# Two projections of a graph attention layer: both made with features on the partitions, values turned back through DRAM

## The chip, the cores and the metric

The kernel runs on one core of one Trainium2 chip. The metric is the device time of one execution in microseconds (us), taken as the median of several runs. A hardware profile of one execution lists the work of each engine: TensorE (PE, with its weight loads as PEld), VectorE (DVE), ScalarE (ACT), GpSimd (POOL) and SyncE (SP), which only issues transfers here.

## The reference, cut to what matters

x is 3327 x 512, adj a 0/1 matrix of 3327 x 3327, W_stack two matrices of 512 x 1024.

```
def gat_layer(x, W, adj):
    Wh, Ws = split(x @ W, 2, axis=-1)        # W = [Wa | Wb]: Wh = x Wa, Ws = x Wb
    a = softmax(Wh @ Ws.T, axis=-1) * adj
    return leaky_relu(a @ Wh + x, 0.01)
y = gat_layer(gat_layer(x, W_stack[0], adj), W_stack[1], adj)
x = layernorm(x + y)
xw = (x > 0) @ sign(weight).T                # then support = adj
x = layernorm(x + relu(adj @ xw))
```

Wh serves twice: as the queries of the scores (Wh Ws^T) and as the values (a Wh). The scores can also be written x (Wa Wb^T) x^T, and the kernel before does so: M = Wa Wb^T is made once for a layer, x itself is the keys, and M applied to x is the queries.

## The kernel before, in words

**Tiles.** The 3327 rows are 26 tiles of 128, taken as 13 pairs (`q`) and as 7 chunks (`c`) of four tiles; the last chunk has two. The 512 features are four groups of 128. Everything in the attention layers is fp32, and one fp32 matmul is two records in the profile. Products of 2x2 blocks are made by the seven-product scheme of Strassen: `seven` (L169) gives seven closures of one chain, each with a product into one of three PSUM banks (X, Y, Z), copies by ScalarE and three additions by VectorE. It needs sums of blocks of both factors: `left_sums` (L204) and `right_sums` (L211), four additions each, S1 to S4 and T1 to T4.

**project (L320)**, for each layer, in three kinds of work per chunk:
- values, Wh with rows on the partitions: x^T is the stationary operand and Wa moves (L408). The result stays in SBUF as `wh[q]`; its sums (`ws_d`) are stored to DRAM by POOL.
- keys: blocks of x^T and their sums (`key_sums`, L236), stored to DRAM as `xs_d` by POOL.
- queries, with features on the partitions: M times x^T (L464); for the half chunk at the end directly, without the scheme (L442). Stored as `gs_d`.

M is made by `product_m` (L304): 16 matmuls of 128x512. It needs Wa and Wb with features of the other side on the partitions. In layer 0 TensorE transposes them at the start of project (`transpose_w`, L257); for layer 1 `load_w_laid` and `turn_w` (VectorE, L283) do it at the end of attention 0.

x of later chunks comes by `load_laid` (L129: four DMAs of 64 KB a tile) and is turned to x^T by VectorE (`turn_x`, L231). The first chunk of layer 0 is transposed by TensorE (L348).

**Order.** A helper `weave` merges lists of closures, each spread evenly. Tiles named `slot` come from one ring of 33 buffers (tag `s`). SP's queue carries all loads in program order, POOL's queue the stores. PSUM has 8 banks: `ch` 3, `acc` 4, `tr` 1.

**attention (L556)** takes 169 steps (g, q) per layer. Scores run 30 steps ahead (`LOOK`), so the last 17 steps have no scores: only the values' products (L822, 7 matmuls a step), with VectorE's shift, running sum and mask (L741, L752, L757) and POOL's sums (L795 to L798). The dictionary `early` places other work by step; toward the end of attention 0 it places the loads and the turning of layer 1's W, M of layer 1 (in the last 14 steps), and the turning of the first chunk of layer 1's x. In steps before 0 the scores' look-ahead runs alone. After layer 1 come the last aggregation and the final normalization.

Of the kernel before, what the change touches and what calls it, by code (L numbers as in the profile page):

```python
# [19 lines left out]
P = 128  # L20
CT = 4
# [9 lines left out]
def kernel(  # L31
# [71 lines left out]
    ba_d = tc.dram_tile([NT, P, D], BF16, name="ba_d")  # L103
    xw_d = tc.dram_tile([NT, P, D], F16, name="xw_d")
# [60 lines left out]

    S1, S2, A11, A12, A21, A22, S3, S4 = range(8)
    B11, B21, B22, T4, T1, T2, T3 = range(7)

    def seven(lane, name, multiply, c11, c12, c21, c22):  # L169
# [5 lines left out]
        def product(i, b, start):  # L175
            if start:
                bank[b] = pool.tile([P, HW], F32, tag=tag, name=f"p{b}_{name}")
            multiply(i, bank[b], start)

        def copied(i, b):  # L180
            if not held:
                two = slot([P, 2, HW], F32, f"h0_{name}"), slot([P, 2, HW], F32, f"h1_{name}")
                held.update(zip(("p1", "p5", "u2", "u3"), (t[:, e] for t in two for e in (0, 1))))
            nc.scalar.copy(held[i], bank[b])
# [19 lines left out]
    def left_sums(a11, a12, a21, a22, s1, s2, s3, s4, eng=nc.vector, between=lambda: None):  # L204
        eng.tensor_tensor(s1, a21, a22, ALU.add)
        eng.tensor_tensor(s2, s1, a11, ALU.subtract)
        between()
        eng.tensor_tensor(s3, a11, a21, ALU.subtract)
        eng.tensor_tensor(s4, a12, s2, ALU.subtract)

    def right_sums(b11, b12, b21, b22, t1, t2, t3, t4):  # L211
        nc.vector.tensor_tensor(t1, b12, b11, ALU.subtract)
        nc.vector.tensor_tensor(t2, b22, t1, ALU.subtract)
        nc.vector.tensor_tensor(t3, b22, b12, ALU.subtract)
        nc.vector.tensor_tensor(t4, b21, t2, ALU.subtract)
# [10 lines left out]
    ch_lane, acc_lane, tr_lane = (ps_ch, "ch"), (ps_acc, "acc"), (ps_tr, "tr")  # L226
    w_rows, w_laid, wT, m_of, wsum_of, x_first, keys_first = ({} for _ in range(7))
# [8 lines left out]
    def key_sums(l, q, a, xT, between=lambda: None):  # L236

        j1, j2 = ts(2 * a, P), ts(2 * a + 1, P)
        s12 = slot([P, 2, 2, P], F32, f"s12_{l}_{q}")
        s34 = slot([P, 2, 2, P], F32, f"s34_{l}_{q}")  # L240
        of = {
            A11: xT[:, 0:2, j1], A12: xT[:, 2:4, j1], A21: xT[:, 0:2, j2],
            A22: xT[:, 2:4, j2], S1: s12[:, 0], S2: s12[:, 1], S3: s34[:, 0],
            S4: s34[:, 1], "s12": s12, "s34": s34,
        }
        left_sums(
            *(of[i] for i in (A11, A12, A21, A22, S1, S2, S3, S4)), between=between
        )
        return of

    def load_w(l, h):

        for k in range(KD):
# [3 lines left out]
    def transpose_w(l, h, k, lane):  # L257
        pool, tag = lane
        pt = pool.tile([P, D], F32, tag=tag, name=f"pwT_{l}_{h}_{k}")
        for d in range(KD):  # L260
            nc.tensor.transpose(pt[:, ts(d, P)], w_rows[l, h, d][:, ts(k, P)], ident)
        wT[l, h, k] = slot([P, D], F32, f"wTs_{l}_{h}_{k}")
        nc.scalar.copy(wT[l, h, k], pt)

    def load_w_laid(l, h, t):

        wt = w_laid[l, h, t] = slot([P, KD, P], F32, f"wl{h}_{l}_{t}")
        for a in range(P // B):
            nc.sync.dma_start(
                out=wt[ts(a, B)],  # L270
                in_=w_stack[l, ts(t, P), h * D + a * P : h * D + (a + 1) * P].rearrange(
                    "(v r) f -> v r f", r=KD
                ),
            )

    def turn_w(l, h, t):

        if t == 0:
            for k in range(KD):
                wT[l, h, k] = slot([P, D], F32, f"wTs_{l}_{h}_{k}")  # L280
        wt = w_laid.pop((l, h, t))
        for k in range(KD):
            nc.vector.transpose(  # L283
                wT[l, h, k].rearrange("p (r c) -> p r c", c=P)[:, :, ts(t, B)],
                wt[:, :, ts(k, B)],
            )

    def sums_w(l):


        wsum_of[l] = ops.tile([P, 4, 2, HD], F32, tag="gs", name=f"wsum_{l}")

        def part(k, half):
            lo, hi = w_rows[l, 0, k], w_rows[l, 0, 2 + k]
            b11, b12, b21, b22 = lo[:, :HD], lo[:, HD:], hi[:, :HD], hi[:, HD:]
            t1, t2, t3, t4 = (wsum_of[l][:, i, k] for i in range(4))
            for to, x1, x2 in ((t1, b12, b11), (t2, b22, t1)) if half == 0 else (
                (t3, b22, b12), (t4, b21, t2)
            ):
                nc.vector.tensor_tensor(to, x1, x2, ALU.subtract)  # L300

        return [lambda k=k, half=half: part(k, half) for half in range(2) for k in range(2)]

    def product_m(l, lane):  # L304

        pm = {}

        def one(d, k):
            if k == 0:
# [5 lines left out]
            if k == KD - 1:  # L315
                copy_out(d, m_of[l][d // 2][:, d % 2], pm[d])
# [1089 lines left out]
```

## Time and profile before

| | |
|---|---|
| median of three runs | 2601.63 us (2599.69 to 2602.28) |
| the profiled execution | 2600.38 us |
| span of the profile | 2598.5 us |
| granted TensorE clock | 0.999 |
| TensorE busy | 2569.2 us, 99% |
| weight loads busy | 2232.3 us, 86% |
| VectorE busy | 2102.4 us, 81% |
| POOL busy | 1102.9 us, 42% |
| ScalarE busy | 789.1 us, 30% |
| DMA | 642.56 MB, mean 247 GB/s |

How to read the lines that follow. A row of the groups has the line of the kernel, the engine, the operation, output and inputs with shapes, the count, then the busy time, the mean duration of one in ns, and the idle time ahead of it with what ended it. A row of the waits has the engine and instruction that waited, what for, and the time in total, how often, and the longest. A row of the timeline has start and duration of a run of equal instructions. A row of the windows has start and end, length, busy time (and count) of PE, PEld, DVE, ACT and POOL, the granted clock as a share, the DMA's busy share, and GB/s. A row of the DMA issues ends with the KB of one and the median us from issue to landing. Layer 0's value products run from 7.6 us of the span to about 185, layer 1's end at about 1392.

### The profile page before, as it was taken

To read this page: it belongs to the slowest core of one execution; us is meant where nothing else is said; L and a number is where in the kernel's file an instruction comes from. 1 tells how busy PE (TensorE), PEld (TensorE's weight loads), DVE (VectorE), ACT (ScalarE), POOL (GpSimd) and SP (SyncE) were. 2 spreads that over 40 slices of the span, in tenths; PEclk is the share of its full clock that TensorE was granted. 3 is DMA by queue.
4 is the path that set the end of the run, shared out by engine and by line. 5 is a ranking of instruction groups with operands and counts; after the bars stand their busy time and mean duration, and the time that the engine had idled before them with its cause. 6 is when DMAs were issued, how large, how long until landed. Compare 5 with 4: busy or idle time off the path is not lost. (4 is left out here: it accounts for less than half of the span.)

```text
span 2598.5 us, 40105 instructions
## 1 busy us (share of the span) xinstructions
PE 2569.2 (99%) x12423; PEld 2232.3 (86%) x12448; DVE 2102.4 (81%) x4442; ACT 789.1 (30%) x1956; POOL 1102.9 (42%) x2048
## 2 busy tenths in 40 slices
PE   9999999999999999999999999999999999999998
PEld 7888888888888888887888888888888888888787
DVE  6756889889898888768875878888888888877976
ACT  3323333333333333221333333333333333222143
POOL 3640344444444444546652144444444444455611
PEclk9999999999999999999999999999999999999999
DMA  6857777877777777787866877777777777778775
GB/s 216 295 193 231 246 247 232 268 235 259 251 240 251 239 247 235 233 259 250 307 235 208 249 239 259 251 258 244 266 258 258 247 256 251 243 261 277 264 247 186
DMA packets 329992, 642.56 MB, mean 247 GB/s; under 512 B 48921, under 2 KB 189555, under 8 KB 329516
## 3 DMA queue, kind: packets, MB, share of 16 engines
q1 hardware_dynamic: 293020, 530.82, 63.1%
q0 software_dynamic: 36752, 109.10, 11.2%
q8 instruction: 102, 1.67, 0.3%
q14 instruction: 118, 0.97, 0.1%
HBM read 530.22 MB, written 109.55 MB: 246 GB/s over the span
## 5 line engine op out<-in xcount | busy, mean ns | idle before, releaser
L588 PE MATMUL pZ<-gs,xs 128*128 128x256 f32 x2496 | 636.1, 379 | 1.3 <-ACT u L605 0.7
L588 PEld LDWEIGHTS pZ<-gs,xs 128*128 128x128 f32 x2496 | 473.6, 190 | 67.5 <-ACT u L605 1.1
L795 POOL TENSOR_TENSOR as<-s 128x128 f32<-128x128 f32 x338 | 161.8, 479 | 846.3 <-DVE s L757 669.4
L822 PE MATMUL acc<-ws,s 128*128 128x256 f32 x1352 | 402.1, 379 | 0.0
L822 PE MATMUL acc<-wh,s 128*128 128x256 f32 x1352 | 355.9, 379 | 0.7 <-DVE s L757 0.4
L822 PE MATMUL acc<-ws,as 128*128 128x256 f32 x1352 | 347.9, 380 | 4.8 <-POOL as L797 4.7
L588 PE MATMUL pY<-gs,xs 128*128 128x256 f32 x1248 | 320.4, 379 | 0.0
L747 ACT ACTIVATE s<-s 128x512 f32<-128x512 f32 x338 | 213.4, 631 | 282.9 <-DVE s L741 281.6
L822 PEld LDWEIGHTS acc<-ws,as 128*128 128x128 f32 x1352 | 256.1, 190 | 46.1 <-POOL as L797 8.9
L822 PEld LDWEIGHTS acc<-wh,s 128*128 128x128 f32 x1352 | 256.5, 190 | 36.9 <-DVE s L757 2.2
L822 PEld LDWEIGHTS acc<-ws,s 128*128 128x128 f32 x1352 | 256.0, 190 | 34.5
L588 PEld LDWEIGHTS pY<-gs,xs 128*128 128x128 f32 x1248 | 236.9, 190 | 32.6 <-ACT p L605 0.3
L658 DVE TENSOR_TENSOR top<-top,s 128x512 f32<-128x512 f32 x286 | 198.9, 710 | 80.9 <-ACT s L645 51.7
L741 DVE TENSOR_TENSOR s<-s,off 128x512 f32<-128x512 f32 x338 | 248.1, 734 | 0.5
L757 DVE TENSOR_TENSOR s<-s,adj 128x512 f32<-128x512 f32 x338 | 238.8, 706 | 8.4 <-DMA adj<-in_adjT_dram 0.5
L752 DVE TENSOR_TENSOR total<-total,s 128x512 f32<-128x512 f32 x312 | 230.3, 738 | 0.0
L605 ACT COPY u<-pZ 128x256 f32<-128x256 f32 x312 | 115.9, 371 | 357.2 <-PE pZ L588 356.6
L797 POOL TENSOR_TENSOR as<-s 128x128 f32<-128x128 f32 x338 | 200.6, 594 | 26.5
L822 PE MATMUL acc<-wh,as 128*128 128x256 f32 x676 | 201.2, 379 | 0.0
L796 POOL TENSOR_TENSOR s<-s 128x128 f32<-128x128 f32 x338 | 187.0, 553 | 27.3
L798 POOL TENSOR_TENSOR as<-s,as 128x128 f32<-128x128 f32 x338 | 178.2, 527 | 26.5
L630 DVE TENSOR_TENSOR s<-p,u 128x256 f32<-128x256 f32 x156 | 66.1, 424 | 143.9 <-ACT u L605 143.3
(224 smaller groups left out, 3866.8 us busy)
## 6 DMA issues: line engine op xcount, KB each, us to landing
ws<-ws_d SPq DMA_DIRECT2D x338, 512.0 KB, 3.7
xs<-xs_d SPq DMA_DIRECT2D x182, 512.0 KB, 6.0
adj<-in_adjT_dram SPq DMA_DIRECT2D x315, 256.0 KB, 4.3
xs<-xs_d SPq DMA_DIRECT2D x156, 384.0 KB, 6.5
gs_d<-gsp POOLq DMA_DIRECT2D x88, 256.0 KB, 3.1
gs<-gs_d SPq DMA_DIRECT2D x74, 256.0 KB, 5.2
adj_d<-ab POOLq DMA_DIRECT2D x169, 112.0 KB, 4.1
ahl<-adj_d SPq DMA_DIRECT2D x78, 224.0 KB, 4.6
```

Of the source, the lines that this page charges most:

```text
L588: nc.tensor.matmul(ch[bank], xs[c, q, a][:, k], gs[c][:, b, k], start=(start and k == 0), stop=(k == 1), skip_group_check=True,)
L605: nc.scalar.copy(ch[name], ch[bank])
L658: nc.vector.tensor_tensor(top[i], top[i], t, ALU.max)
L741: nc.vector.tensor_tensor(s, s, off[g].to_broadcast([P, 2, HW]), ALU.subtract)
L747: nc.scalar.activation(sc[g, q], sc[g, q], AF.Exp)
L752: nc.vector.tensor_tensor(total[g], total[g], sc[g, q], ALU.add)
L757: nc.vector.tensor_tensor(s, s, adj[g, q], ALU.mult)
L795: nc.gpsimd.tensor_tensor(s3, a11, a21, ALU.subtract)
L796: nc.gpsimd.tensor_tensor(a21, a21, a22, ALU.add)
L797: nc.gpsimd.tensor_tensor(s2, a21, a11, ALU.subtract)
L798: nc.gpsimd.tensor_tensor(s4, a12, s2, ALU.subtract)
L822: nc.tensor.matmul(acc[g][i // 2][:, i % 2], a[i], b[i], start=(q == 0 and i % 2 == 0), stop=(q == NQ - 1), skip_group_check=True,)
```

## The change

M is no longer made. Both halves of x W are made with features on the partitions: W's blocks are the stationary operand and x^T moves (`products`, called for `wsT`, the keys, and then for `whT`, the queries). Each call is two chains of seven products, 28 matmuls, over all columns of a chunk; in the last chunk the four blocks are 128 columns wide instead of 256 (`width`). ScalarE puts W's columns into the order that the blocks need (`part_w`), VectorE makes W's sums. Keys are blocks of Ws^T with their sums, queries Wh^T with theirs.

The values are the same numbers as the queries, but needed with rows on the partitions. `turn_rows` turns each tile by two VectorE transposes of 128x256 into a buffer `wr` (three copies), from which four DMAs on SP store it to a new DRAM tensor `wh_d`. Later three DMAs on SP load it into `wh[q]` (`load_values`), and VectorE makes its sums: for the first six pairs within project (at chunks 2 to 4), for the other seven in attention's steps −29 to −3. At the start of layer 0 the loads of x and W alternate. For layer 1, Wb is loaded, ordered and summed in the last steps of attention 0; the work with M, and the turning of W, leave those steps.

`left_sums` and `right_sums` now return lists of closures. The diff, cut to its core (of removed functions only the first lines and those that are named here; the rest of project's old loop is left out):

```diff
+    wh_d = [tc.dram_tile([NT, P, D], F32, name=f"wh_d{l}") for l in range(L)]
...
-    def transpose_w(l, h, k, lane):
...
-            nc.tensor.transpose(pt[:, ts(d, P)], w_rows[l, h, d][:, ts(k, P)], ident)
-        wT[l, h, k] = slot([P, D], F32, f"wTs_{l}_{h}_{k}")
-        nc.scalar.copy(wT[l, h, k], pt)
...
-    def load_w_laid(l, h, t):
...
-    def turn_w(l, h, t):
...
-    def product_m(l, lane):
...
-            nc.tensor.matmul(
-                pm[d], wT[l, 0, k][:, ts(d, P)], wT[l, 1, k], start=(k == 0), stop=(k == KD - 1)
-            )
...
+    def part_w(l, h, k, to):
+        nc.scalar.copy(
+            to.rearrange("p (e c) -> p e c", c=P),
+            w_rows.pop((l, h, k)).rearrange("p (c e) -> p e c", e=KD),
+        )
+    def left(lo, hi, sums):
+        of = {A11: lo[:, :, :HD], A12: hi[:, :, :HD], A21: lo[:, :, HD:], A22: hi[:, :, HD:]}
+        of.update({i: sums[:, e] for e, i in enumerate((S1, S2, S3, S4))})
+        return of
+    def left_w(of):
+        return left_sums(*(of[i] for i in (A11, A12, A21, A22, S1, S2, S3, S4)))
+    def width(c):
+        return HW if len(halves_of(c)) == 2 else P
+    def right_x(c, xT, t):
+        w = width(c)
+        lo, hi = xT[:, 0:2], xT[:, 2:4]
+        of = {B11: lo[:, :, :w], B21: hi[:, :, :w], B22: hi[:, :, w : 2 * w]}
+        of.update({i: e[:, :, :w] for i, e in zip((T1, T2, T3, T4), t)})
+        return of, right_sums(
+            of[B11], lo[:, :, w : 2 * w], *(of[i] for i in (B21, B22, T1, T2, T3, T4))
+        )
+    def load_values(l, q, b12):
+        nc.sync.dma_start(out=wh[q][:, 0], in_=wh_d[l][2 * q][:, :HD])
+        nc.sync.dma_start(
+            out=wh[q][:, 1:3], in_=wh_d[l][2 * q + 1].rearrange("p (a n) -> p a n", a=2)
+        )
+        nc.sync.dma_start(out=b12, in_=wh_d[l][2 * q][:, HD:])
...
+        def sums_x(c):
+            if c < 2 or c == NC - 1:
+                t = [slot([P, 2, HW], F32, f"xt_{l}_{c}_{i}") for i in range(4)]
+            else:
+                if "one" not in spare:
+                    spare["one"] = ops.tile([P, 2, HW], F32, tag="xs1", name=f"xt_{l}")
+                units = [spare_of[l][:, 2 * i : 2 * i + 2] for i in range(7)] + [spare["one"]]
+                t = units[:4] if c % 2 == 0 else units[4:]
+            of_x[c], do = right_x(c, xTs[c], t)
+            return do
+        spare = {}
+        wa = pre.tile([P, KD, D], F32, tag="wa", bufs=1, name=f"wa_{l}")
+        m = pre.tile([P, KD, D], F32, tag="m", bufs=1, name=f"wb_{l}")
+        asum = pre.tile([P, 4, 2, HD], F32, tag="msum", bufs=1, name=f"wasum_{l}")
...
+            load_x(0, (0, 1))
+            load_w(l, 1, (0, 1))
+            load_x(0, (2, 3))
+            load_w(l, 1, (2, 3))
+            load_w(l, 0)
+            spare_of[l] = ops.tile([P, 14, HW], F32, tag="gs", name=f"spare_{l}")
+            wsum_of[l] = ops.tile([P, 4, 2, HD], F32, tag="gs", name=f"wbsum_{l}")
+            wb_of[l] = m[:, 0:2], m[:, 2:4]
...
+        def products(c, name, of_w):
+            w = width(c)
+            n = len(halves_of(c))
+            made = [slot([P, 2, HW], F32, f"{name}_{l}_{c}_{i}") for i in range(2 * n)]
+            blocks = made if n == 2 else [
+                t[:, :, i * P : (i + 1) * P] for t in made for i in range(2)
+            ]
+            of = of_x[c]
             def multiply(et):
                 def go(i, bank, start):
                     for k in range(2):
                         nc.tensor.matmul(
+                            bank, of_w[LEFT[i]][:, k, ts(et, P)], of[RIGHT[i]][:, k],
                             start=(start and k == 0), stop=(k == 1), skip_group_check=True,
                         )
                 return go
+            chains = [
+                seven(lane, f"{name}_{l}_{c}_{et}", multiply(et), *(t[:, et] for t in blocks), w=w)
+                for et, lane in enumerate((ch_lane, acc_lane))
+            ]
+            return chains, list(zip(made[:n], made[n:]))
+        def keys(q, lo, hi):
...
+            one, two, three, four = left_sums(
+                a11, a12, a21, a22, s12[:, 0], s12[:, 1], s34[:, 0], s34[:, 1]
             )
+            return [
+                lambda: (one(), two(), out(S1, 2, s12), out(A11, 1, a11), out(A12, 1, a12)),
+                lambda: (three(), four(), out(S3, 2, s34), out(A21, 1, a21), out(A22, 1, a22)),
+            ]
+        def queries(c, made):
+            def out(i, t):
+                nc.gpsimd.dma_start(out=gs_d[l][c][:, i], in_=t)
+            if len(made) == 1:
+                return [lambda: [out(i, t) for i, t in zip((B11, B21), made[0])]]
+            (b11, b21), (b12, b22) = made
+            t = [slot([P, 2, HW], F32, f"gsp_{l}_{c}_{i}") for i in range(4)]
+            one, two, three, four = right_sums(b11, b12, b21, b22, *t)
+            return [
+                lambda: (one(), two(), out(B11, b11), out(B21, b21), out(B22, b22)),
+                lambda: (three(), four(), out(T1, t[0]), out(T2, t[1]), out(T3, t[2]),
+                         out(T4, t[3])),
+            ]
+        def turn_rows(t, lo, hi):
+            wr = pre.tile([P, P // B, P], F32, tag="wr", bufs=3, name=f"wr_{l}_{t}")
+            to = wr.rearrange("p r (u k) -> p r k u", u=B)
+            for side, half in enumerate((lo, hi)):
+                nc.vector.transpose(
+                    to[:, :, 2 * side : 2 * side + 2],
+                    half[:, :, ts(t % 2, P)].rearrange("p k (r v) -> p r k v", v=B),
+                )
+            for a in range(P // B):
+                nc.sync.dma_start(
+                    out=wh_d[l][t][:, ts(a, P)].rearrange("(r v) f -> v r f", v=B),
+                    in_=wr[ts(a, B)],
+                )
+        def begin_values(q):
+            rows34[q] = slot([P, 2, HD], F32, f"t34_{l}_{q}")
+            load_values(l, q, rows34[q][:, 0])
+        def sum_values(q):
+            t12, t34 = slot([P, 2, HD], F32, f"t12_{l}_{q}"), rows34.pop(q)
+            for do in right_sums(
+                wh[q][:, 0], t34[:, 0], wh[q][:, 1], wh[q][:, 2],
+                t12[:, 0], t12[:, 1], t34[:, 0], t34[:, 1],
+            ):
+                do()
+            nc.gpsimd.dma_start(out=ws_d[l][q][:, 0:2], in_=t12)
+            nc.gpsimd.dma_start(out=ws_d[l][q][:, 2:4], in_=t34)
+        rows34 = {}
+        weights = [lambda k=k: part_w(l, 0, k, wa[:, k]) for k in range(KD)] + left_w(of_a)
         if l == 0:
+            transpose_first(acc_lane)
+            for k in range(KD):
+                part_w(l, 1, k, m[:, k])
+            t, b = sums_x(0), left_w(of_b)
+            for do in t[:2] + b[:2]:
                 do()
+            weights = [b[2], t[2], b[3], t[3]] + weights
         else:
+            weights += [
+                lambda e=e: nc.scalar.copy(m[:, 2 * e : 2 * e + 2], wb_of[l][e]) for e in range(2)
+            ]
+        rest = []
         for c in range(NC):
+            new = range(len(tiles_of(c + 1))) if c + 1 < NC else ()
+            chains, made = products(c, "wsT", of_b if c or l == 0 else first_b)
+            turns = [lambda a=a: transpose_x(c + 1, a) for a in new[:2]]
+            if c == 0:
+                turns = weights + turns
+            weave(*chains, rest, turns)
+            load_x(c + 2)
+            rest = [do for a, e in enumerate(made) for do in keys(c * CT // 2 + a, *e)]
+            turns = [lambda a=a: transpose_x(c + 1, a) for a in new[2:]]
             if c + 1 < NC:
+                turns.append(lambda: later.extend(sums_x(c + 1)))
+                turns += [lambda: later.pop(0)()] * 4
+            later = []
+            old = [q for q in (2 * c - 4, 2 * c - 3) if 0 <= q < ROWS]
+            turns += [lambda q=q: sum_values(q) for q in old]
+            chains, made = products(c, "whT", of_a)
+            weave(*chains, rest, turns)
+            rest = queries(c, made)
+            for a, e in enumerate(made):
+                rest += [
+                    lambda t=t, e=e: turn_rows(t, *e) for t in half_tiles(c * CT // 2 + a)
                 ]
+            for q in (2 * c - 2, 2 * c - 1):
+                if 0 <= q < ROWS:
+                    begin_values(q)
...
+        def begin_values(q):
+            t = ws["new", q] = att.tile([P, 4, HD], F32, tag="ws", bufs=WS, name=f"wn_{l}_{q}")
+            load_values(l, q, t[:, 2])
+        def sum_values(q):
+            t = ws.pop(("new", q))
+            for do in right_sums(
+                wh[q][:, 0], t[:, 2], wh[q][:, 1], wh[q][:, 2], *(t[:, i] for i in range(4))
+            ):
+                do()
+            nc.gpsimd.dma_start(out=ws_d[l][q], in_=t)
+        for n, q in enumerate(range(ROWS, NQ)):
+            at = 1 - LOOK + 4 * n
+            assert at + 2 < 1 - WS
+            early[at] = [(0.9, lambda q=q: begin_values(q))]
+            early.setdefault(at + 2, []).append((0.75, lambda q=q: sum_values(q)))
...
-            for i, do in enumerate(product_m(l + 1, ch_lane)):
-                early.setdefault(end + 3 + i * n // (KD * KD), []).append(
-                    (0.3 + 0.4 * (i % 2), do)
-                )
...
+            place(end + 3, 0.9, lambda: load_w(l + 1, 1))
+            place(end + 4, 0.2, begin_w)
+            for k in range(KD):
+                place(end + 6 + k, 0.3, lambda k=k: part_w(
+                    l + 1, 1, k, wb_of[l + 1][k // 2][:, k % 2]
+                ))
+            place(end + 10, 0.6, lambda: parts.extend(
+                left_w(left(*wb_of[l + 1], wsum_of[l + 1]))
+            ))
+            for i in range(4):
+                place(end + 10 + i, 0.65, lambda: parts.pop(0)())
+            place(n - 10, 0.95, lambda: load_w(l + 1, 0))
             for a in range(CT):
-                early.setdefault(n - 9 + a, []).append((0.9, lambda a=a: load_first(a)))
-                early.setdefault(n - 4 + a // 2, []).append((0.45, lambda a=a: turn_first(a)))
-            for a in range(CT // 2):
-                early.setdefault(n - 2, []).append((0.6 + a / 10, lambda a=a: keys_of_first(a)))
+                place(n - 9 + a, 0.9, lambda a=a: load_first(a))
+                place(n - 5 + a // 2, 0.45, lambda a=a: turn_x(x_first[l + 1], a, laid.pop(0)))
+            place(n - 3, 0.4, sums_of_first)
             for i in range(4):
-                early.setdefault(end + 7 + i, []).append((0.65, lambda: parts.pop(0)()))
+                place(n - 3 + i // 2, 0.6 + i % 2 / 10, lambda: parts.pop(0)())
```

## The prediction

> **What bounds the kernel now.** I read the page first (engine shares), then TensorE's waits, its groups by form, its timeline at the start, and the windows of the two stages that the change touches.
>
> ```profile
> PE 2569.2 (99%) x12423; PEld 2232.3 (86%) x12448; DVE 2102.4 (81%) x4442; ACT 789.1 (30%) x1956; POOL 1102.9 (42%) x2048
> ```
>
> ```profile
> PE acc L822 <- POOL as L797: 4.7, 7, 1.2
> PE pxt L348 <- DMA xr<-in_x_dram: 3.6, 1, 3.6
> ```
>
> TensorE is busy in 99% of the span and its longest waits sum to under 10 us, so a record taken from its stream shortens the span by that record's pitch, as long as VectorE (81% on average, more in places) keeps up.
>
> ```profile
> L312 PE MATMUL pm<-wTs,wTs 128*128 128x512 f32 x64 | 31.1, 592 | 0.0
> L442 PE MATMUL pg<-xT,m 128*128 128x256 f32 x64 | 15.1, 379 | 0.0
> L442 PEld LDWEIGHTS pg<-xT,m 128*128 128x128 f32 x64 | 12.2, 190 | 1.7
> L261 PEld LDWEIGHTS pwT<-ident,w 128*128 128x128 f32 x16 | 1.8, 140 | 1.4 <-ACT wTs L263 1.3
> ```
>
> ```profile
> 3.59 3.83 PE L348 MATMUL pxt<-ident,xr 128*128 128x128 f32 x16 [3.59 <-DMA xr<-in_x_dram]
> 7.57 1.20 PE L408 MATMUL pZ_wh<-wa,xT 128*128 128x256 f32 x4
> ...
> 12.96 0.63 PE L261 MATMUL pwT<-ident,wa 128*128 128x128 f32 x4
> 13.43 1.03 PE L408 MATMUL pZ_wh<-wsum,s 128*128 128x256 f32 x4
> ...
> 35.07 3.60 PE L312 MATMUL pm<-wTs,wTs 128*128 128x512 f32 x8
> 38.50 1.89 PE L464 MATMUL pZ_g<-xT,m 128*128 128x256 f32 x8
> 40.23 1.89 PE L464 MATMUL pX_g<-xT,m 128*128 128x256 f32 x8
> ```
>
> Mean durations overlap, so I price by start to start. Eight 256-wide records take 40.23 − 38.50 = 1.73 us, .216 each; eight 512-wide take 38.50 − 35.07 = 3.43 us, .429 each; four W transposes, between 12.96 and 13.43, .47 us, .118 each. An fp32 matmul of the program is two records.
>
> **The change on TensorE.** *Full chunk:* before, two value pairs and the queries are 14+14+28 matmuls; after, keys and values 28+28. Both are 112 records of .216 = 24.2 us: nothing. *M, layer 1:* 32 of the 64 records of L312 go: 32 × .429 = **−13.7**; they stood in attention 0's last 14 steps. *Start of layer 0:* before, the first value product is at 7.57 and the first chunk's queries end at 38.50 + 56 × .216 = 50.6. After, x and W loads alternate (about .76 us per 256 KB at 343 GB/s), so x's transposes end at about 8.4, their copies at 9.5, ScalarE's reordering of W (four copies of .59, the row of L263) and the first sums let the first product go at about 10.4. Then 112 records: 10.4 + 24.2 + 1 for a cold start = 35.6; **−15.0**. This holds layer 0's M and its 32 transposes. The 1 us is a weighing. The row of L348 is 424 ns, that of L261 282: TensorE has two prices at the start, the higher after its wait. "TensorE: Matmul & The Clock Gate", section "HAM oscillation — how this bites in real kernels", says that TensorE must not idle over about 3.4 us; my gap is 2 us. By the rule nothing is lost, by the cold row perhaps 2 us; I take 1. *Last chunk:* before, 16+14 matmuls, 60 records × .216 = 12.95 us; after, 56 matmuls, 112 records, of 128 columns. No fp32 product that narrow is in the trace. Bounds: .107 (half of .216), 12.0 us; .190 (the weight load's row), 21.3 us. The page's section "Back-to-back issue gap" speaks against this part: a stream of loads and matmuls is spaced by both, and at 128 columns stands at 81 ns where the columns alone want 56, i.e. the load sets the pace. Taken alone that makes 21.3 us (+8.3 a layer), the columns alone 12.0 (−1.0). The nearest row is the transposes': pitch .118 beside a load of 140, i.e. .84 of the load; .84 × .190 = .16 per record, 17.9 us: +5.0 a layer, **+9.9**.
>
> **VectorE.** Per full chunk (24.14 us) it has about 19.4 us of work. What is new is that each tile is turned back to rows by two 128x256 transposes. That form is bounded by
>
> ```profile
> L231 DVE STREAM_TRANSPOSE xT<-xr 128x512 f32<-128x512 f32 x48 | 52.2, 1097 | 0.1
> L692 DVE STREAM_TRANSPOSE top<-top 128x256 f32<-128x256 f32 x26 | 11.5, 441 | 0.5
> ```
>
> (strided, twice as wide, .55; contiguous .44); it has L231's pattern, so .53, and 8 × .53 = 4.3 a chunk. With 12 bank additions (4.4), turning x (4.1), key sums (3.0), x sums (2.6), query sums (2.6) and value sums (3.0, only at chunks 2 to 4) I get 21.0 us in chunks 1 and 5, 24.0 in 2 to 4: 99% of it. So it is level with TensorE for three chunks of each layer; lag beyond 6.9 us (a PSUM bank's addition is needed five products of 1.72 us later, less one) reaches TensorE one to one.
>
> **The stores of turned values.** The buffer `wr` has 3 copies, so a chunk's fourth turn waits for the first's four DMAs of 64 KB on SP's queue. The weave puts those turns .42 and .92 through a stage of 12.07 us, three product pairs apart: 5.2 to 6.0, say 5.5. VectorE stands by x = landing + 1.1 (the turn) − 5.5, and behind it stand that chunk's bank additions, which free TensorE's banks. Landings, in the rows of the busiest stage before:
>
> ```profile
> 60.00:84.00 24.00, 24.00 (x113) 21.13 (x112) 18.58 (x40) 7.44 (x20) 13.91 (x23) 1.00 1.00 355
> ```
>
> ```profile
> xr<-in_x_dram SPq DMA_DIRECT2D x16, 64.0 KB, 6.6
> ws_d<-t POOLq DMA_DIRECT2D x4, 256.0 KB, 6.7
> xs_d<-xT POOLq DMA_DIRECT2D x8, 128.0 KB, 8.0
> ```
>
> There 8.5 MB moved in 24 us with the DMA full (share 1.00). After, chunks 2 and 3 move about 7.8 MB each (keys' blocks and sums 2, queries 1.8, values' sums 1, x 1, and turned values out and in, 1 each): nearly as full, twice over. Bounds 2.3 us (x loads in 38 to 60) and 14.8 (an attention load queued in 60 to 84); by the nearest rows 7.3. Then x = 2.9, over chunks 2 to 4 8.7, less 6.9: 1.8 a layer, **+3.6**. POOL issues about as many DMAs as before. SP issues 143 more per layer; past the x loads of c+2 these are 16 stores waiting for turns, so the loads stand up to half a stage later, covered by a whole chunk (24 us).
>
> **Borders.** At the end of project the first xs load stands on SP behind the last two tiles' stores and lands about 1 us after its need (0 to 3): **+2** for two layers. At the end of attention 0, without M, seven steps last 3.02 us each (14 records) = 21.1; VectorE's shift, running and masked (2.2 a step), turning x (4.4), sums of x (2.8) and W (2.8) are 25.3; less what may lag, **+3** (0 to 5). Windows of that stage before, and of layer 1's, which has no M:
>
> ```profile
> 1180.00:1200.00 20.00, 19.14 (x81) 14.67 (x80) 19.37 (x31) 3.16 (x5) 17.09 (x32) 1.00 0.76 257
> 2420.00:2440.00 20.00, 18.01 (x87) 13.59 (x86) 19.27 (x38) 4.10 (x7) 12.62 (x24) 1.00 0.86 306
> ```
>
> With VectorE near 19.3 of 20 TensorE loses 1 to 2 us. Before's own losses there (.26 in the 20 us ahead of that window, .86 in it) go with W's turning: **−1.1**.
>
> **Sum:** −15.0 − 13.7 − 1.1 + 9.9 + 3.6 + 2 + 3 = −11.3. The span of 2598.5 becomes 2587.2, the profiled execution 2600.38 − 11.3 = 2589.1. The median of the runs is 1.25 above the profiled one: **2590**.
>
> **Rivals.**
> *Faster still:* the narrow records go at their columns' pace (.107) and stores land at 6.6 us. For: the transposes at .118 under a load of 140. Against: the fp32 load is 190. The last chunk gives −1.9 instead of +9.9, the stores nothing: −26.7, **2575**.
> *The same:* the narrow records are bound by their loads, .190: +16.7 instead of +9.9; **2597**, and with VectorE's borders at their upper ends (+5 and +6) 2603. For: the rule above. Against: the transposes' row.
> *Slower:* VectorE stands at `wr` for the stores. Per layer the loss is 3x + 2 max(0, x − 3) − 6.9, as chunks 1 and 5 have 3 us to spare. The gain is gone at x = 4.1, a landing of 8.5 us; it is slower than noise from about 9. At 12 us, x = 7.6, 25 a layer: 2598.5 − 14.9 + 50, **2636**. For: the DMA is as full as in 60 to 84 for two chunks in a row, and there stores took up to 8.0; SP's queue puts x loads and attention's loads beside them. Against: the same stage before was absorbed with TensorE at 24.00 of 24.
>
> That M doesn't go is no rival: no instruction of it is left.
>
> **How the numbers follow.** Forecast .47 (its own range 2582 to 2597), faster still .14, the same .15, slower .24. A measurement tells from no change at about 0.2%, 5.2 us: below 2596.4 is faster, above 2606.8 slower. The forecast's case lies below 2596.4 but for .03: faster .58, same .18, slower .24. The range 2573 to 2625 leaves out .06 below and .13 above, in the slower case's further half.
>
> **What would show it.** Right: no records of L312's or L261's kind; chunk 0's second projection ends at 35 to 36; narrow records at .15 to .17 start to start; windows of 24 us in chunks 1 to 5 with TensorE at 23 or more of 24 and VectorE at 21 to 24; the turned stores landing at 6.5 to 8.5 us. Wrong: TensorE's waits name a VectorE bank addition whose own wait is a `wr` store; VectorE's turn at 1 us instead of .53; the wait for values loaded into `wh` or for the first xs or gs load longer than 3 us at the start of attention.

## The result: 26 us slower

The changed kernel takes 2628.03 us (2627.12 to 2629.62, four runs) against 2601.95 us; the ratio is 1.0102, with a 95% interval of 1.0085 to 1.012. The profiled execution has a span of 2625.7 us, 27.2 more than before. The forecast was 2590, the range 2573 to 2625.

The page after, and then TensorE's waits (total, times, longest):

```profile
PE 2554.6 (97%) x12456; PEld 2227.5 (85%) x12456; DVE 2141.6 (82%) x4528; ACT 802.9 (31%) x1986; POOL 1095.4 (42%) x2030
```

```profile
PE pZ L531 <- DVE whT L190: 14.1, 2, 7.3
PE pZ L531 <- DMA xs<-xs_d: 13.1, 6, 5.7
PE pX_wsT L370 <- DVE whT L190: 5.7, 4, 2.6
...
PE acc L765 <- POOL as L740: 5.6, 7, 1.2
PE pX L531 <- DVE s L579: 3.2, 2, 1.6
```

TensorE's busy time falls by 14.6 us and its idle time grows by 42, but 14.6 is not what the change takes off. By count and pitch its records fall by 32.1 us: 64 of 512 columns, 32 transposes and 120 of 256 columns go, 224 of 128 columns come. The busy time hides this, since the trace before lacks 25 records of 512 columns near its end (12423 where 12448 weights were loaded), and since records after a wait are slow (last section). The three waits on top did not exist before. They belong to few moments, as landmarks in the traces show (us from the start of the span; the last column is the kernel of the fifteenth experiment, told below):

| landmark | before | changed | difference | 15th |
|---|---|---|---|---|
| first product of project 0 | 7.6 | 11.4 | +3.9 | 11.2 |
| chunk 1's first product | 50.6 | 37.5 | −13.1 | 37.8 |
| 201st record of layer 0's scores | 227.6 | 237.8 | +10.2 | 214.3 |
| first values' product of layer 0 | 278.3 | 291.4 | +13.1 | 268.5 |
| last score of layer 0 | 1164.5 | 1177.5 | +13.0 | 1153.4 |
| last values' product of layer 0 | 1232.7 | 1239.3 | +6.6 | 1215.2 |
| first values' product of layer 1 | 1484.8 | 1511.9 | +27.1 | 1470.3 |
| end | 2598.5 | 2625.7 | +27.2 | 2585.7 |

The gain of the start (13.1) is lost again between chunk 1 and the first scores, twice over; the gain at the end of attention 0 (6.4) is lost three times over in layer 1, between there and the first values' product. From the first values' product to the last score each attention takes as long as before. This is the border of layer 0, TensorE's timeline first, then VectorE's, then SP's:

```profile
171.12 1.06 PE L370 MATMUL pZ_whT<-xT,wa 128*128 128x128 f32 x8
172.01 1.06 PE L370 MATMUL pX_whT<-xT,wa 128*128 128x128 f32 x8
...
173.80 1.06 PE L370 MATMUL pY_whT<-xt,wasum 128*128 128x128 f32 x8
182.15 1.22 PE L531 MATMUL pZ<-gs,xs 128*128 128x256 f32 x2 [7.29 <-DVE whT L190]
183.16 1.91 PE L370 MATMUL pZ_whT<-xt,wasum 128*128 128x128 f32 x8
...
198.52 2.05 PE L531 MATMUL pZ<-gs,xs 128*128 128x256 f32 x4 [5.74 <-DMA xs<-xs_d]
```

```profile
168.33 2.05 DVE L422 STREAM_TRANSPOSE wr<-whT 128x256 f32<-128x256 f32 x4
...
180.89 1.08 DVE L422 STREAM_TRANSPOSE wr<-whT 128x256 f32<-128x256 f32 x2 [8.87 <-DMA wh_d<-wr]
181.81 0.47 DVE L190 TENSOR_TENSOR whT<-pX_whT,h_whT 128x128 f32<-128x128 f32 x2
```

```profile
161.61 0.34 SPq L513 DMA_DIRECT2D gs<-gs_d  x1
162.00 1.71 SPq L522 DMA_DIRECT2D xs<-xs_d  x2
169.47 23.80 SPq L427 DMA_DIRECT2D wh_d<-wr  x24
193.32 0.93 SPq L522 DMA_DIRECT2D xs<-xs_d  x2
```

SP first issued attention's loads of gs (1.8 MB) and of the first xs (0.9 MB), then the stores of chunk 5. The four stores of the first turned tile were issued from 169.5 on and landed at 178.4 to 180.8, behind these loads. Only then was its buffer free; VectorE had stood 8.87 us at the fourth tile, with the addition that empties TensorE's bank behind it, and TensorE stood 7.29. SP was done with the 24 stores of chunks 5 and 6 only at 193.3, and the second xs load stood behind them: TensorE waited again, 5.74 us.

The 24 stores took 23.8 us of SP's time, but their own issues only 12.5. For 4.2 us, to 188.2, SP waited for the turns of the last tiles, which VectorE did late. Most of the rest were waits for older transfers to land: the store at 175.20 went out when the first xs load had landed (175.18), the next at 177.22 after the second (177.21). Counted over the traces of all kernels but the seventh, where SP's landings are not recorded, no transfer from SP or ScalarE is issued while eight of these two engines' transfers together are outstanding, and none from POOL while eight of its own are. So 2.7 MB of loads at the head of a queue hold back the stores behind them also by keeping three of these places, until 172.9 to 177.2. Whether the program or the chip sets the eight is not shown here.

### The profile page after: what moved, and what is told of

Read it like the earlier page. It is cut to its first block, busy times and chain, and to the rows that moved or that the text cites. A ratio compares the mean times of both kernels' runs of the same rounds, so it can differ in the third digit from the quotient of the medians.

```text
span 2625.7 us, 40583 instructions
## 1 busy us (share of the span) xinstructions
PE 2554.6 (97%) x12456; PEld 2227.5 (85%) x12456; DVE 2141.6 (82%) x4528; ACT 802.9 (31%) x1986; POOL 1095.4 (42%) x2030
## 5 line engine op out<-in xcount | busy, mean ns | idle before, releaser
L700 DVE TENSOR_TENSOR s<-s,adj 128x512 f32<-128x512 f32 x338 | 238.3, 705 | 10.2 <-POOL as L740 1.5
```

What stands on the lines that cost most here:

```text
L700: nc.vector.tensor_tensor(s, s, adj[g, q], ALU.mult)
```

## The experiments

Each kernel is the changed one with the edit that is shown, on top of others where that is said. Its time is the median of its runs, and the ratio is to the kernel before on the same chip. The chips differ between experiments, so small steps are best read from the ratios.

**1. The turned tiles in the big ring.**

```diff
-            wr = pre.tile([P, P // B, P], F32, tag="wr", bufs=3, name=f"wr_{l}_{t}")
+            wr = slot([P, P // B, P], F32, f"wr_{l}_{t}")
```

> The changed kernel, with the turned tiles in the ring of 33 buffers instead of three of their own; nothing else. Theory A (VectorE stands at the three buffers for the stores, and TensorE's banks behind it): the waits of VectorE for stores go, chunks 1 to 5 lose under 2 us a layer instead of 6.5 and 4.2, the border loses 7 us less a layer; 2628 - 9 - 14 = about 2605. Rival B (VectorE is simply full in chunks 2 to 4): the chunks lose as before, only the border gains; about 2614. Rival C (SP's queue: stores stand ahead of attention's second pair of loads): the border's second wait (5.7 and 4.4 us for the loads of xs) stays or grows.

Measured 2622.6, ratio 1.008 (1.0064 to 1.0097): only 5 us gained. VectorE's waits for the stores are gone, and project 0 ends at 176.9 instead of 186.9. But the other wait has taken most of what that gave:

```profile
PE pZ L531 <- DMA xs<-xs_d: 26.1, 6, 11.7
PE pX_whT L370 <- DVE wsT L190: 6.5, 2, 4.0
```

The wait for the second xs load grew from 5.7 to 11.7 us, and in layer 1 from 4.4 to 10.8, since TensorE now arrives 9.5 us sooner at a load that lands only 3.6 us sooner. The second row is new in this size: in chunk 5 VectorE waits for tiles of x, which also stand on SP behind stores. So the chunks of layer 0 lose 5.8 us, hardly less than the 6.5 of the changed kernel, where theory A expected under 2. A and C hold, in series: what the buffers no longer hold up, SP's queue does.

**2. and 3. The stores from ScalarE's queue,** with three buffers, and with the ring.

```diff
-                nc.sync.dma_start(
+                nc.scalar.dma_start(
                     out=wh_d[l][t][:, ts(a, P)].rearrange("(r v) f -> v r f", v=B),
```

> The changed kernel, with the turned tiles stored from ScalarE's DMA queue instead of SP's; three buffers as in the changed kernel. Theory C (the stores share SP's queue with the 1.8 MB of gs and 0.9 MB of xs that attention loads first, so they land late, and the next xs stands behind them): the stores land in under 5 us at the border instead of 9.9, both border waits shrink to under 3 us a layer, about 2628 - 25 = 2603, and the chunks gain too. Theory A alone: the stores land no sooner, VectorE still stands 8 us at the border, only the xs wait of 10 us in all goes: about 2618. Against both: the stores' issue costs ScalarE time, which delays the copies out of TensorE's banks.

> Both together: turned tiles in the ring and stored from ScalarE's queue. If A and C are two causes that add: 2628 - 24.8 (VectorE at the buffers, chunks and border) - 10.1 (xs) = about 2593. If one contains the other, no better than the better one of the two single edits.

Measured 2687.3, ratio 1.0325 (1.0307 to 1.0342), and 2687.8, 1.0335 (1.0317 to 1.0352): some 60 us slower than the changed kernel. The view of the store's line in the second kernel tells why; its last rows are who waited for it (us, times):

```profile
L427 ACTq DMA_DIRECT2D wh_d<-wr x208: 309/457/1945, 44.3 to 1472.5; - x104
...
  ACT h_wsT L187: 70.5, 15
  ACT wsT L200: 34.9, 6
```

An issue costs ScalarE as much as SP (0.457 us by the median, up to 1.9; the 208 sum to 111.5), and ScalarE's copies, which empty TensorE's banks, stand behind it in order: 105 us of waits. The expectation had named this as what spoke against both. Not all of it is issuing. A row of ScalarE's waits from 20 to 190 us names tiles of x that SP loads and that ScalarE's copies do not read; this fits the eight outstanding transfers that the two engines share:

```profile
ACT wsT L200 <- DMA xr<-in_x_dram: 17.9, 3, 6.0
```

**4. No turning. 6. Turning, but no stores.** In both, the values are loaded from rows of the input, so what is multiplied in a @ Wh is not Wh, and no load of values waits for a store any more. The fourth leaves out VectorE's transposes and the stores; the sixth has the transposes (into the ring) and leaves out the stores.

```diff
             for a in range(P // B):
-                nc.sync.dma_start(out=wh_d[l][t]...)
```

> The changed kernel without the turning of values and without their stores; the values are loaded from rows of the input instead (as many bytes), so the output is not the reference's. All theories: what is lost in project and at its borders by the turning alone is gone: 2628 - 10.7 - 33.5 = about 2584. What then still stands against the forecast's terms lies elsewhere: the end of attention 0 (6 us) and the first attention steps (5 us).

> The changed kernel with VectorE turning every tile (into the ring), but nothing stored; values loaded from rows of the input, so the output is not the reference's. It has all of VectorE's work and none of the stores. If VectorE's fullness in chunks 2 to 4 costs nothing by itself: as without the turning, 2585. If VectorE is over full there: 3 chunks x up to 4.3 us a layer less what may lag, up to 2600.

Measured 2585.4, ratio 0.9944 (0.9928 to 0.9961), and 2586.1, 0.9936 (0.9919 to 0.9953). This settles two things. All of project's loss comes from the stores and what stands around them; without them the change gives 15 to 17 us. It does not tell the stores from the loads that wait for them. And B falls: VectorE's fullness costs nothing by itself, as the sixth kernel's windows for chunks 3 and 4 show (PE, PEld, DVE, ACT, POOL busy of 24 us; then clock, DMA share, GB/s):

```profile
84.00:108.00 24.00, 24.00 (x113) 21.13 (x112) 22.72 (x48) 7.27 (x21) 13.63 (x24) 1.00 0.84 283
108.00:132.00 24.00, 24.00 (x113) 21.11 (x113) 22.71 (x48) 7.28 (x21) 13.15 (x24) 1.00 0.66 232
```

VectorE is at 22.7 of 24, and TensorE at 24.00.

**5. The second and third xs loads from POOL's queue,** on top of the ring.

```diff
-                nc.sync.dma_start(out=t[:, :n], in_=xs_d[l][q][:, a : a + n])
+                eng = nc.gpsimd if c == 0 and q in (1, 2) else nc.sync
+                eng.dma_start(out=t[:, :n], in_=xs_d[l][q][:, a : a + n])
```

> The kernel with the turned tiles in the ring (the first experiment, 2622.6), and attention's second and third pair of xs loads of the first chunk issued from POOL's queue instead of SP's, where 24 stores stand ahead of them. If these stores make the border's remaining wait (11.65 and 10.84 us for xs), it goes: 2622.6 - 20 = about 2602. Rival: the wait only moves to the next loads behind the stores on SP (the fourth pair of xs, values for wh): about 2612.

Measured 2613.0, ratio 1.0048 (1.0031 to 1.0064): half of the 20 us. The rival is right that the wait partly moves on: VectorE now waits 9.2 us for the first loaded values, whose stores are late too.

**7. One store per tile, gathered by the loads,** on top of the ring. `wr` is stored as it lies, 256 KB at once; eight loads of 64 KB per pair sort it.

```diff
-            for a in range(P // B): ...
+            nc.sync.dma_start(out=wh_d[l][t], in_=wr.rearrange("p r f -> p (r f)"))
...
+        for a in range(4):
+            nc.sync.dma_start(out=first, in_=cols_of(2 * q, a))
+            nc.sync.dma_start(out=wh[q][:, 1 + a // 2, ts(a % 2, P)], in_=cols_of(2 * q + 1, a))
```

> The kernel with the turned tiles in the ring, and the layout in DRAM turned round: one store of 256 KB a tile, as it lies in the buffer, instead of four of 64 KB; the values are gathered by eight loads of 64 KB a pair instead of three. SP issues 26 stores and 104 loads a layer instead of 104 and 39. If the time of SP's queue at the border (24 issues one after the other, 10 us and more) is the cause: xs waits of 3 us instead of 11.65 and 10.84, about 2606; less what 56 loads in attention's first 30 steps delay (0 to 5). If bytes on the DMA rings are the cause and not the number of issues: the waits stay, 2620.

Measured 2666.9, ratio 1.0255 (1.0238 to 1.0272), worse than either case that was expected. Nearly as many issues (130 a layer instead of 143) remain, and a gathering load takes SP .62 to .69 us by the median of its two lines and up to 4.9. TensorE's largest wait is behind VectorE's sums of values:

```profile
PE pZ L529 <- DVE wn L209: 20.4, 4, 6.7
PE pZ_wsT L372 <- ACT h_wsT L187: 19.5, 4, 7.6
PE pZ L529 <- DMA xs<-xs_d: 17.5, 9, 3.0
```

The second row has its cause in the ring: a turned tile keeps its buffer until its store has landed, the stores stand on SP behind 16 loads of values per chunk, and ScalarE waited for their landing before it had buffers to copy to (25.4 us in two waits, 15.9 in four). That the loads' size and place make the whole difference is argued; it was not tested apart.

**8. Layer 1's Wa loaded sooner.**

```diff
-            place(n - 10, 0.95, lambda: load_w(l + 1, 0))
+            place(end + 7, 0.95, lambda: load_w(l + 1, 0))
```

> The changed kernel with the load of layer 1's Wa (1 MB) placed right after Wb's, 9 steps before its place in the changed kernel. The end of attention 0 loses 6 us more than before: 1.8 wait for ws loads, 0.5 for x sums. If Wa's load beside x's is what delays these: 2628 - 2 = 2626. If VectorE's chain alone sets the steps once M no longer fills them: no change.

Measured 2629.5, ratio 1.0107 (1.009 to 1.0124): no gain.

**9. to 11. The issues spread over queues.** All with the ring; two of a tile's four stores from POOL; the last seven pairs' values loaded from POOL. The ninth has the second and third xs from POOL, the tenth the second from ScalarE and the third from POOL, the eleventh the second from ScalarE and the third from SP.

```diff
-                nc.sync.dma_start(
+                (nc.sync if a < 2 else nc.gpsimd).dma_start(
...
-            load_values(l, q, t[:, 2])
+            load_values(l, q, t[:, 2], nc.gpsimd)
...
+                eng = nc.scalar if c == 0 and q == 1 else nc.sync      # the eleventh
```

> The ring of the first experiment and xs from POOL of the fifth (2613), with the issues spread further: of each tile's four stores two go from SP and two from POOL; the values for the last seven pairs (21 loads a layer) are loaded from POOL's queue too. SP then issues 30 DMAs per chunk instead of 38, and 12 instead of 24 stores at the border. If the time of SP's queue is what is left: chunk 4's late x (2.9 and 4.8 us) goes and most of the border's and first steps' 8 to 10 us a layer: 2613 - 18 = about 2595. Floor, with no store at all: 2586. Rival: POOL's queue becomes the late one (its xs loads stand behind its own stores): about 2610.

> As the split, with attention's second pair of xs loads issued from ScalarE's queue, ahead of the copies of the last chunk, since on POOL they stand behind the last stores. If that order matters: 3 to 5 us a layer below the split, about 2590; if not, the same as the split.

> As the tenth kernel, but the third pair of xs loads issued from SP, where 12 stores stand ahead of it, and not from POOL, where it stood behind a load of values that waits for their stores (TensorE then waits 10.7 and 9.0 us for xs). If the place in the queue is the cause: 2610 - 10.7 - 9.0 + 2 for what is left = about 2592, 10 us below the kernel before. If the bytes ahead in the DMA engines are the cause, the wait stays: 2610.

Measured 2614.8 (ratio 1.0051, 1.0038 to 1.0065), 2609.6 (1.0035, 1.0021 to 1.0048) and 2605.7 (1.002, 1.0011 to 1.0029). In all three chunks 1 to 5 lose nothing any more: with 30 issues per chunk on SP, tiles of x and stores come in time. At the border a wait of the same size stayed and changed its name: 11.5 us in the ninth for the second xs, behind POOL's own stores; 10.7 in the tenth for the third, behind a load of values that waits for its stores; in the eleventh, VectorE's wait for the values themselves:

```profile
DVE wn L209 <- DMA wn<-wh_d: 9.9, 1, 9.9
```

**12. to 15. Where the last seven pairs' values are loaded and summed,** all on top of the eleventh. The changed kernel loads at steps −29, −25, ... and sums two steps later. The twelfth starts at −24, every third step; the thirteenth at −24, every second; the fourteenth is the thirteenth with Wb's work at the end of attention 0 two steps sooner; the fifteenth loads at −26, every third step, and sums four steps later.

```diff
-            at = 1 - LOOK + 4 * n
-            early[at] = [(0.9, lambda q=q: begin_values(q))]
-            early.setdefault(at + 2, []).append((0.75, lambda q=q: sum_values(q)))
+            at = 4 - LOOK + 3 * n                                          # the fifteenth
+            early.setdefault(at, []).append((0.7, lambda q=q: begin_values(q)))
+            early.setdefault(at + 4, []).append((0.75, lambda q=q: sum_values(q)))
```

> As the eleventh kernel, but the last seven pairs' values are loaded and summed 5 to 0 steps later in attention's look-ahead (from step -24, every third step, in place of -29, every fourth). There VectorE stood 9.9 and 11.7 us at the first of these sums for values that were stored only at the border, and TensorE 6.8 and 5.9 us behind it. If this is the last of the round trip's stalls: 2605.7 - 12 = about 2593, faster than the kernel before by 0.3%. If the wait only moves on (to xs, or to the adjacency's loads): 2602 to 2606.

> As the twelfth kernel, with the sums of the last seven pairs' values on every second step from -22 to -10, between the steps in which VectorE halves blocks of the adjacency, not on them. In the twelfth the border lost only 5 and 3 us, but four waits of about 3.3 us stood at X banks behind VectorE in the look-ahead, 11 us a layer where before lost 3. If sums and blocks falling together are the cause: 2605.8 - 12 = about 2594, 8 us below the kernel before. If the round trip's loads as such make VectorE late: 2602 to 2606.

> As the thirteenth kernel, with layer 1's Wb loaded, ordered and summed two steps sooner at the end of attention 0, out of the last seven steps. There VectorE has 25.3 us of work by rows for 21.1 of TensorE's, and 8 us are lost where the kernel before lost 1.6. If VectorE's fullness there is the cause: 2 us less than the thirteenth; if it is the loads of ws behind those of W and x: no change.

Measured 2605.8 (ratio 1.0016, 1.0007 to 1.0024), 2620.3 (1.0073, 1.0059 to 1.0087) and 2621.5 (1.0083, 1.0069 to 1.0097). In the twelfth the border of layer 0 has no wait of TensorE left, but the gain is spent in the look-ahead, in three waits of 2.9 to 3.4 us. The thirteenth speaks against sums and blocks falling together as the cause: apart from each other, and closer in a row, they cost more. POOL's timeline in the twelfth shows the cause:

```profile
188.27 0.57 POOL L283 DMA_DIRECT2D wn<-wh_d  x1
...
198.64 0.56 POOL L924 DMA_DIRECT2D ws_d<-wn  x1 [9.32 <-DVE wn L209]
...
199.23 0.54 POOL L279 DMA_DIRECT2D wh<-wh_d  x1
...
210.41 0.55 POOL L924 DMA_DIRECT2D ws_d<-wn  x1 [8.00 <-DVE wn L209]
...
211.74 0.54 POOL L279 DMA_DIRECT2D wh<-wh_d  x1 [0.25 <-issue]
```

POOL stands at the store of a sum until VectorE has made it; the next pair's load stands behind that store, so it is issued too late for its own sum, and VectorE waits 5 us for it, as in this row of 205 to 230 us:

```profile
DVE wn L209 <- DMA wn<-wh_d: 5.1, 1, 5.1
```

The fifteenth takes the load out of that circle; the sums stay on the steps of the twelfth:

> As the twelfth kernel, but each of the last seven pairs' values is loaded 4 steps ahead of its sum instead of 2 (loads at steps -26 to -8, every third, sums at -22 to -4), so that on POOL's queue a load stands ahead of the store of the sum before it. In the twelfth POOL stood 8 to 9 us at each of these stores until VectorE had made the sum, the next load was issued only then, VectorE waited 5 us for it, TensorE 2.9 to 3.4 us. If that circle is the cause of the look-ahead's 11 us a layer: 2605.8 - 14 = about 2592, faster than the kernel before by 0.35%. If not: 2602 to 2606.

Measured **2588.0** (2586.9 to 2590.45), ratio 0.9952 (0.9939 to 0.9966): 12.6 us faster than the kernel before and 40 faster than the changed one, with the same arithmetic, the same bytes and the same number of DMAs. POOL still stands at the store of a sum, but the loads for the next pair are ahead of it:

```profile
188.68 0.56 POOL L283 DMA_DIRECT2D wn<-wh_d  x1 [0.58 <-PE pY L532]
...
189.94 0.56 POOL L279 DMA_DIRECT2D wh<-wh_d  x1 [0.22 <-issue]
...
199.48 0.54 POOL L924 DMA_DIRECT2D ws_d<-wn  x1 [7.92 <-DVE wn L209]
```

From 185 to 290 us VectorE no longer waits for a loaded value, and of TensorE's three such waits a layer (1.9 to 3.4 us) one is left in each. Its TensorE waits, and the window of the border that cost 17 us:

```profile
PE pX L532 <- DVE s L580: 5.8, 2, 2.9
PE pxt L314 <- DMA xr<-in_x_dram: 5.6, 2, 3.8
PE acc L766 <- POOL as L741: 5.5, 7, 1.2
```

```profile
180.00:200.00 20.00, 20.00 (x94) 17.58 (x93) 9.35 (x19) 6.45 (x18) 8.85 (x17) 1.00 1.00 350
```

The same window of the changed kernel:

```profile
180.00:200.00 20.00, 12.11 (x56) 10.67 (x57) 7.06 (x19) 2.92 (x9) 5.01 (x8) 0.76 0.77 231
```

The DMA is fuller in the fast kernel (share 1.00, 350 GB/s) than in the slow one (0.77, 231): with the same bytes in all, the transfers were not too many; they stood on the wrong queues and in the wrong order. Which of the fifteenth kernel's edits (ring, split stores, xs from ScalarE, values from POOL, later sums) it could do without was not tested.

## Why the prediction was wrong

By its own steps. Excess below is start to start of TensorE's records beyond .216 (256 columns) or .112 (128).

| step | forecast | measured | by |
|---|---|---|---|
| start of layer 0 | −15.0 | −13.1 | first product at 11.4, not 10.4; cold records cost 1.9, not 1, behind gaps of 1.9 and 1.75 us |
| M of layer 1 | −13.7 | −13.7 | no such record left |
| last chunk's narrow records | +9.9 | −0.9 | 171.12 to 172.01: .112 each, 12.5 us a layer |
| stores within chunks 1 to 5 | +3.6 | +10.7 | excess 6.5 and 4.2 |
| border project to attention | +2 | +33.5 | excess 17.2 and 16.3 |
| first steps of attention | 0 | +5.0 | excess 3.1 and 1.9 more than before |
| end of attention 0 | −1.1 + 3 | +6.0 | excess 7.6 against 1.6 |
| sum | −11.3 | +27.5 | span +27.2 |

**The step that failed** is the border: "the first xs load stands on SP behind the last two tiles' stores and lands about 1 us after its need". The first xs load went ahead of the stores, not behind them. With gs it put 2.7 MB in front of chunk 5's stores, so that VectorE stood at `wr` and TensorE behind it (7.3 us), and the second xs load then stood behind the last six tiles' stores, 24 instead of 8 (5.7 us). The prediction had each piece, but let the buffers matter only within chunks and the queue only for its last two tiles. The price of an issue was missing too. It was in the trace before, .43 us by the median for the loads of x and up to 1.7; the prediction counted SP's 143 more DMAs a layer and costed them at nothing. The first of its signs of being wrong came true as written: TensorE's waits name a bank addition of VectorE, whose own wait is a `wr` store.

**The stores within chunks.** The mechanism of the *slower* rival is right, VectorE stands at `wr`; its place is right only in part. The rival put it into chunks 2 to 4 through full DMA engines, and priced a landing of 12 us at 2636; the border cost three times as much as all chunks. Over all 208 stores the median landing is 2.1 us, below the 2.3 that I took as the lower bound. What counts is the first tile's stores of a chunk, which no median shows: those of chunk 3 were issued from 123.2 on, behind six loads of values on SP, and landed 7.2 down to 3.3 us later, where VectorE stood for them:

```profile
131.15 1.15 DVE L422 STREAM_TRANSPOSE wr<-whT 128x256 f32<-128x256 f32 x2 [5.21 <-DMA wh_d<-wr]
```

VectorE stood at the fourth tile of chunks 1 to 5 of layer 0 for 1.9, 5.0, 5.2, 2.3 and 8.9 us. The allowance was wrong as well: the stand of 5.2 us reached TensorE with a wait of 2.6, where 6.9 were to be absorbed. At the border the same four landed after 8.9 to 10.2 us, and the rival's "a landing of 8.5 us" was passed there.

**VectorE's work** was right in size: 104 transposes in 55.5 us, .53 each as estimated, 22.7 of 24 us without the stores; and it is no bound, as the prediction's sum assumed and the sixth run shows.

**The narrow records** go at their columns' pace, .112. The 128x128 weight loads beside them still have rows of 190 ns, so .84 of a load was the wrong measure. The Trainium skill ("TensorE: Matmul & The Clock Gate", "Back-to-back issue gap"), which the prediction read as loads setting the pace at 128 columns, does not fit these fp32 records: they are not held up by their loads. That is 10.8 us in favour of the forecast, and no merit of it; without this error it would have missed by 49.

**The end of attention 0** lost 6.0 where 1.9 were forecast. Loading Wa sooner didn't help, nor did moving Wb's work two steps up (excess 9.0 in the fourteenth run, 8.0 in the thirteenth). The waits name the adjacency's work on POOL (2.7 us, 1.0 before), late loads of ws (2.2) and a sum of x (0.7). That M's records had filled such waits is argued only; the cause stays open. It remains in the fifteenth run (8.0).

With the queues put in order the change gives 2588, where 2590 was forecast. That it gains was forecast rightly; that the numbers meet is in part luck. The narrow records gave 10.8 us more than forecast, the start 2 less, and the look-ahead and the end of attention 0 lose 14 us more than before in the fifteenth kernel, where the forecast allowed 7.5 for stores and borders.

## What to carry to other kernels

A DMA that waits for an engine's result blocks everything behind it on its queue, so price a moved transfer by the queue: what is issued ahead of it (here .3 to 1.9 us each), how many bytes that is, how many transfers are outstanding, and what stands behind. Where a round trip through DRAM crosses a border between stages, write down the order of each queue at that border before estimating anything else. When one stall is removed and the time stays, look for the next wait of the same size under another name: here there were five in series (buffers, SP, POOL's xs, the sums' place, POOL's circle), and the first four gave 22 us of the 40 and left the kernel slower than the one before; only the last brought it ahead.

## What was not expected of the hardware

Issuing a DMA occupies the queue's engine for about .45 us (medians of the turned tiles' stores: SP .446, ScalarE .457; POOL .54 to .57), and now and then up to 1.9 us. In the changed kernel such long issues of SP occur only while earlier transfers of SP are outstanding; with none, the longest is .40.

A wait also costs speed afterwards: after TensorE's 7.29 us at the border eight narrow records took 1.71 us (183.16 to 184.87) instead of .89, with the granted clock at .76 in 180 to 200. Of the excess of 17.2 us there, 13.0 are waits and 4 are slow records. A shorter wait can do it too: after 2.61 us in project 0 (138.0 to 140.6) the granted clock was .53 from 141 to 144, and slow records cost 1.8 us more, although the wait is below the 3.4 us that the prediction took from the Trainium skill ("TensorE: Matmul & The Clock Gate", "HAM oscillation — how this bites in real kernels"). Not each wait of this length does: after 2.50 us in attention 0 (1194.3 to 1196.8) nothing was lost.
